# Attention scores of 16-wide heads in sixteen 32x32 array tiles per group, and another order in one pool of buffers

## The chip, the cores and the metric
The kernel runs on one core of a Trainium2 chip. Its time is the device time of one launch in microseconds (us); a profile is one further execution, recorded by the hardware profiler. TensorE (PE) multiplies; it is a systolic array of 128 rows and 128 columns that can be divided into tiles, each of which takes its own weights and its own stream. The profile keeps its weight loads (PEld) apart from its streams (PE). VectorE (DVE), ScalarE (ACT) and GpSimd (POOL) work elementwise beside it, and SyncE (SP) mainly issues transfers.

## The reference, cut to what matters
Two decoder layers over `x` of 8 sequences, 256 rows, 256 features, all in fp32. Layer 0 has self-attention with rotary positions, cross-attention and an expert-choice feed-forward; layer 1 has causal self-attention, cross-attention with a null key, and a feed-forward of eight routed experts and a shared one. The three attentions with heads of 16 compute

```python
# 16 heads of 16; layer 0 self, layer 0 cross (bias b, masked keys), layer 1 self (causal)
scores = einsum('bhqd,bhkd->bhqk', q, k) * scale      # 256 queries x 256 keys a head
attn   = softmax(scores)
out    = einsum('bhqk,bhkd->bhqd', attn, v)           # v of 16 features a head
```

and the feed-forward at the end has the shared expert, whose second weights the other edit touches:

```python
shared_aD = silu(x_aD @ ws1_DF) * (x_aD @ ws3_DF) @ ws2_FD     # F = 704
```

## The kernel before, in words
**Attention units.** `units` is a list of 24: per pair of sequences two self-attentions and two cross-attentions of layer 0, and after those of layer 0 eight causal self-attentions of layer 1. Each unit has a `Core`, and each `Core` runs four steps. `queries` splits a step into `c`, which half of the 16 heads, and `kt`, which 128 of the 256 keys.

**One step.** `scores` makes the group of products named `st` for eight heads (L334). Heads of 16 lie in strips of `HP` = 32 partitions; strip `r` of `kT` holds the keys of two heads side by side in its 32 rows, and `qm` holds the queries twice, `m` = 0 and 1, each time masked to one of the two heads. One matmul per strip thus gives two heads: a contraction of 32 rows, 128 keys as its 128 columns of weights, and 2 x 256 queries as its stream of 512. The four strips are four 32x128 tiles of the array, and each writes its own 2 KB bank of the tile `st`. In the causal units the second key half (`kt` = 1) takes only the second 128 queries, so its stream has 256 columns. There are 24 x 4 = 96 such groups, 16 of them with 256 columns. ACT then turns the group into exponentials in two instructions of two banks each (`pT`, L345), and in causal units POOL blanks the upper triangle (L350). `values` multiplies by the padded values (`o`, L371): eight matmuls on 128x32 tiles. Where `kt` is 1, DVE divides.

**Order.** The pool `scp` that holds `st` has one buffer of four banks, so a group of scores can't start before ACT has read the group before it. The order of the engines is written out by hand under `manual_schedule`, and between the groups stand pieces of the neighbouring units and of the expert layer, put there by `beside(n, k, at, ...)`. The loop is

```python
for k in range(4):
    if k < 3:
        u.core.scores(k + 1)
    elif n + 1 < len(units):
        units[n + 1].core.scores(0)
    run(n, k, True)
    u.core.values(k)
    run(n, k, False)
```

so PE gets the scores of the next step, then (`run(n, k, True)` holds few pieces) the values of this one, then the pieces beside. Those pieces use other tile shapes: `product` (L276) makes two column tiles of 128x64, `product4` (L282) four of 128x32; `transposed` (L291) and the products `hx` (L1079) take the whole array. `lg` is the group of expert logits, four calls of `product4` in one place; `cs`, `rps`, `qk` and `y` are other small groups, `xn` and `xnx` are normalised rows made on DVE, `g` are the gates of the expert layer.

**An fp32 matmul is two.** The profile records two passes for one fp32 matmul of the code, each with its own weight load. The 384 matmuls of L334 are 768 streams and 768 loads in the trace.

**The late stage.** `null_cross_attention` loops `b` over the 8 sequences. At the last `b` it closes the pools of its own weights (`wproj.close()`), opens the pool `late` in their place and calls `load_shared(late)`. That allocates `ws13` and lets `w_in` issue its two DMAs on SP and a small copy on POOL (L1028 to L1030), allocates the two buffers `mid0` and `mid1`, and then `ws2`, each of the three with a small memset on POOL (`ended`, L1035) for its unused end. `w_out` later issues the two DMAs of `ws2` on SP (L1039, L1040), behind the stores that `rest` and `reciprocals` have put on that queue. `hidden_shared` is the first reader of `ws13` (`hx`, L1079); `divide` on POOL and `outward` with its products `wo` (L276) follow. `ws2` is first read from 970.7 us on (`out`, L1663).

The pool takes over addresses that earlier buffers held. In bytes of a partition these were `vx` (values of the last cross-attention, read by the products `ox`, L1470) at 162,464 to 170,656, `wkv_x` at 170,656 to 203,424 and `wq_x` at 203,424 to 211,616. Before the change `ws13` lies at 168,768 to 180,544, over the end of `vx`; then `mid0` from 180,544, `mid1` from 192,832 and `ws2` at 205,120 to 211,264.

Of the kernel before, what the change touches and what calls it, by code (L numbers as in the profile page):

```python
# [29 lines left out]
F32 = mybir.dt.float32  # L30
# [9 lines left out]
P = 128  # L40
B, S, D = 8, 256, 256
NT = B * S // P
H, HD = 16, 16
HP = 32
# [6 lines left out]
NFC = len(FCH)  # L51
# [106 lines left out]
def plain(  # L158
# [4 lines left out]
    nc = tc.nc  # L163
# [100 lines left out]
    def layernorm_T(b, work, mm, bufs=2):  # L264

        xn = work.tile([P, 2, D], F32, tag="xn", name="xn", bufs=bufs)
        mv, rs = norm_stats([x[:, 2 * b + t, :] for t in range(2)], 1e-5, small, "ln")
        for t in range(2):
            last = normed(xn[:, t, :], x[:, 2 * b + t, :], mv, rs, t)
        return last, transposed(xn, work, mm, "xnT", bufs=bufs)  # L270
# [45 lines left out]
    class Core:  # L316
# [9 lines left out]
        def scores(self, step):  # L326


            c, kt, q0 = self.queries(step)
            n = S - q0  # L330
            st = scp.tile([P, 4, 2, S], F32, tag="sc", name="st")
            for r in range(4):
                rows = slice(HP * r, HP * r + HP)
                nc.tensor.matmul(  # L334
                    st[:, r, :, :n],
                    self.kT[rows, c, bass.ts(kt, P)],
                    self.qm[rows, :, c, q0:],
                    start=True,
                    stop=True,
                )  # L340
            pTs = []
            for k in range(2):
                pT = work.tile([P, 2, 2, S], F32, tag="pT", name="pT", bufs=4)
                kb = {} if self.bias is None else {"bias": self.bias[:, kt : kt + 1]}
                nc.scalar.activation(  # L345
                    pT[:, :, :, :n], st[:, 2 * k : 2 * k + 2, :, :n], AF.Exp, scale=self.scale, **kb
                )
                if self.causal:

                    nc.gpsimd.affine_select(  # L350
                        out=pT[:, :, :, :P],
                        in_=pT[:, :, :, :P],
                        compare_op=ALU.is_ge,
                        fill=0.0,
                        base=0,
                        pattern=[[0, 2], [0, 2], [1, P]],
                        channel_multiplier=-1,
                    )
                pTs.append(pT)
            self.exps[step] = pTs  # L360
# [488 lines left out]
    def context(b):  # L849
        t = ctxs.tile([P, CTX // P, S], F32, tag="ctxT", name="ctxT")  # L850
        nc.sync.dma_start(t, a["ctx_T"][b].rearrange("(c p) t -> p c t", p=P))
        return t

    def key_room():
        return kvs.tile([P, nc8, S], F32, tag="kT", name="kTx")
# [61 lines left out]
    for k in range(4):  # L917
# [7 lines left out]
    start = begun + (  # L925
        (0, 2, EARLY), (0, 3, 40), (0, 3, 41), (1, 0, 70), (1, 2, 70),
        (1, 3, 70), (2, 0, 15), (2, 1, 5), (2, 2, 70), (2, 3, 20), (2, 3, 70), (3, 0, 70), (3, 1, 45),
        (3, 2, 70), (3, 3, 85),
    )
# [95 lines left out]
    def w_in(pool, src1, src3, name):  # L1025

        t = pool.tile([P, 2, 2 * FF + tail], F32, name=name, tag=name)
        nc.sync.dma_start(t[:, :, :FF], src1.rearrange("(c p) f -> p c f", p=P))  # L1028
        nc.sync.dma_start(t[:, :, FF + tail :], src3.rearrange("(c p) f -> p c f", p=P))
        nc.gpsimd.tensor_copy(t[:, :, FF : FF + tail], t[:, :, 2 * FF :])  # L1030
        return t

    def ended(t):

        nc.gpsimd.memset(t[tail:, full, :], 0.0)  # L1035
        return t

    def w_out(t, src):
        nc.sync.dma_start(t[:, :full, :], src[: full * P].rearrange("(c p) d -> p c d", p=P))  # L1039
        nc.sync.dma_start(t[:tail, full, :], src[full * P :])  # L1040
        return t
# [5 lines left out]
    shared = {}  # L1047
# [5 lines left out]

    def load_shared(pool):

        shared["ws13"] = w_in(pool, a["L1_ffn_ws1_DF"], a["L1_ffn_ws3_DF"], "ws13")

        shared["mid_s"] = [ended(pool.tile([P, NFC, 2 * S], F32, name=f"mid{i}")) for i in range(2)]
        shared["ws2"] = ended(pool.tile([P, NFC, D], F32, name="ws2"))

    def hidden(mid, first, n, pair, silu):

# [126 lines left out]
    def routed_norm(b, work):  # L1189

        xn = work.tile([P, 2, D], F32, tag="y", name="xne", bufs=1)
        mv, rs = norm_stats([x[:, 2 * b + t, :] for t in range(2)], 1e-5, small, "ln")
        for kept, v in zip(norms[b], (mv, rs)):
            nc.gpsimd.tensor_copy(kept, v)
        for t in range(2):
            normed(xn[:, t, :], x[:, 2 * b + t, :], mv, rs, t)
        return xn

    def routed_rows(b, xn, work):
        transposed(xn, work, mm, "", shared["xnT"][:, :, bass.ts(b, S)])  # L1200
# [87 lines left out]
    def null_cross_attention(phase):  # L1288
# [42 lines left out]
        def sums_of_rows(rows, n, name, apart):  # L1331


            def block(i, j):
                return rows[:, n * j : n * (j + 1), bass.ts(i, P)]

            sw = wsum.tile([P, 4 if apart else 3, n, P], F32, tag=name, name=name)
            s1, s2, s4 = (sw[:, i] for i in range(3))
            s3 = sw[:, 3] if apart else block(1, 0)
            nc.vector.tensor_tensor(s1, block(1, 0), block(1, 1), ALU.add)  # L1340
            nc.vector.tensor_tensor(s2, s1, block(0, 0), ALU.subtract)
            nc.vector.tensor_tensor(s4, block(0, 1), s2, ALU.subtract)
            nc.vector.tensor_tensor(s3, block(0, 0), block(1, 0), ALU.subtract)
            return block(0, 0), block(0, 1), s4, block(1, 1), s1, s2, s3
# [223 lines left out]
        for b in range(B):  # L1568
            more = b + 1 < B
            if more:  # L1570
                ctxT = context(b + 1)
            oT, den, rest = weighted(kT, v, qT)
            if more:
                _, xnT = layernorm_T(b + 1, work, mm, 1)
                if b:
                    xe = routed_norm(b - 1, work)
                of_ctx = sums_of_rows(ctxT, CTX // P // 2, "sw", False)
            else:
                xe = routed_norm(b - 1, work)
                rest()  # L1580

                wproj.close()
                late = ctx.enter_context(tc.tile_pool(name="mids", bufs=1, side="right"))
                load_shared(late)
                sums = phase.enter_context(tc.tile_pool(name="sums", bufs=1, side="right"))
                order.enter_context(tc.manual_schedule(engines={mybir.EngineType.PE}))
            if more:
                order.enter_context(tc.manual_schedule(engines={mybir.EngineType.PE}))
            if b:
                routed_rows(b - 1, xe, work)  # L1590
            if more:
                of_x = sums_of_rows(xnT, 1, "swq", True)
                kT, v, qT = key_room(), value_room(), query_room()
                k7 = seven("k7", of_ctx, w_terms(kv_blocks, 0), kT, False)
                v7 = seven("v7", of_ctx, w_terms(kv_blocks, 1), v, True)
                q7 = seven("q7", of_x, w_terms(q_blocks, 0), qT, False)
                next(k7)
                rest()
            rs, old = reciprocals(b, den, en), en
            if b == 1:  # L1600
                in_range()
            if not more:
                w_out(shared["ws2"], a["L1_ffn_ws2_FD"])
                routing_tables(late)
            if more:

                for made in (k7, k7, v7, k7, k7, k7, v7, v7, q7, v7, q7, v7, v7, q7):
                    next(made)
            else:
                first = hidden_shared(0, pair, lambda n: spare()[:, 0, :n])  # L1610
                for i in range(4):
                    next(first)
                    if i == 0:
                        routed_scores(b - 1)
                shared["of_w"] = sums_of_shared(*(sums.tile([P, full * P], F32, name=f"tws{i}") for i in range(4)))
            divide(oT, rs, (nc.gpsimd, nc.gpsimd if more else nc.vector))
            outward(b, oT, old)
            if more:
                next(q7), next(q7)
                if b:  # L1620
                    routed_scores(b - 1)
                next(q7)
                en = null_key(xnT)
            else:
                for _ in first:
                    pass
            order.close()
# [1230 lines left out]
```

## Time and profile before

| what | value |
|---|---|
| median of 3 runs | 1198.14 us (1196.61 to 1200.52) |
| profiled execution, its own time | 1198.71 us |
| its span | 1197.0 us |
| PE busy | 1135.5 us, 95% |
| weight loads | 706.5 us, 59% |
| DVE, ACT, POOL busy | 47%, 37%, 35% |
| `st` streams (L334) in the chain that ended last | 4% of the span |
| `hx` (L1079) in that chain | 3% of the span |

The span runs from the first to the last recorded instruction; the 1.7 us between it and the execution's own time are start and end. The busy time of PE counts any moment in which at least one stream runs, so streams of several tiles beside each other count once. The row `PEclk` gives the clock that the throttle granted to TensorE in tenths, 9 for nine tenths or more, in 40 slices of 29.9 us. Durations of single instructions are in nanoseconds, and a line of the timeline is a run of equal instructions: its start in us, its length in us, the engine, the line, the operation, the tile of the array (rows by columns), the shape of weights or result, and the count.

### The profile page before, as it was taken

How to read it: one execution, taken by the hardware profiler on the slowest of the kernel's cores; microseconds unless marked ns; L12 is line 12 of the kernel's file. 1: busy time of each engine (PE TensorE's matmuls, PEld its weight loads, DVE VectorE, ACT ScalarE, POOL GpSimd, SP SyncE). 2: the span in 40 equal slices, each digit the busy share in tenths (PEclk: the TensorE clock that was granted, in tenths of full speed). 3: DMA queues.
4: the chain of work that ended last, by engine and by line, in shares of the span. 5: the costliest groups of instructions: out<-in, count | busy, mean ns of one | idle time of the engine just before them, and what ended most of it. 6: DMA issues, size and time to landing. Idle time of an engine off the chain costs nothing.

```text
span 1197.0 us, 31939 instructions
## 1 busy us (share of the span) xinstructions
PE 1135.5 (95%) x13788; PEld 706.5 (59%) x13788; DVE 566.2 (47%) x1564; ACT 447.5 (37%) x696; POOL 417.6 (35%) x482
## 2 busy tenths in 40 slices
PE   6898899998899999999999999999998999999996
PEld 2334444454445454666676767666664576888864
DVE  5465878778685643824241424242324473222213
ACT  3666665665443541314141414141413230222220
POOL 3245365455655730314141414141415114100013
PEclk9999999999999999999999999999998999999999
DMA  7046232130200600020202010101103007799924
GB/s 226 1 133 204 91 119 92 54 122 2 84 2 17 233 3 19 2 54 2 54 2 54 6 50 10 46 19 37 24 15 105 5 30 305 277 414 394 392 73 129
DMA packets 51446, 116.78 MB, mean 98 GB/s; under 512 B 8272, under 2 KB 36416, under 8 KB 46944
## 3 DMA queue, kind: packets, MB, share of 16 engines
q1 hardware_dynamic: 45120, 98.90, 24.0%
q0 software_dynamic: 3456, 12.73, 2.9%
q10 hardware_dynamic: 2720, 3.02, 0.7%
q8 instruction: 110, 1.80, 0.6%
q14 instruction: 40, 0.33, 0.1%
HBM read 104.00 MB, written 27.93 MB: 110 GB/s over the span
## 4 chain that ended last, share of the span: by engine, by line
PE 76%; POOL 7%; issue 6%; DVE 6%; ACT 4%; DMA 1%; SPq 0%; POOLq 0%; ACTq 0%; DVEq 0%
PE h L276 7%; PE k L276 6%; PE v L276 6%; PE wo L276 5%; PE ox L1470 5%; PE stx L1431 5%; PE st L334 4%; PE out L1846 4%; PE o L371 3%; PE out L1663 3%; PE h L1079 3%; PE qk L282 3%; PE q L276 3%; ACT pT L345 2%; PE den L1446 2%
## 5 line engine op out<-in xcount | busy, mean ns | idle before, releaser
L345 ACT ACTIVATE pT<-st 128x1024 f32<-128x1024 f32 (+1 forms) x128 | 110.7, 919 | 64.3 <-PE st L334 64.3
L371 PE MATMUL o<-pT,padv 128*32 128x256 f32 (+1 forms) x1536 | 99.7, 370 | 4.3 <-POOL pT L350 4.2
L371 PEld LDWEIGHTS o<-pT,padv 128*32 128x32 f32 x1536 | 40.6, 109 | 86.2 <-issue 37.5
L1437 POOL TENSOR_TENSOR both<-pTx 128x512 f32<-128x512 f32 x64 | 81.2, 1296 | 29.0 <-ACT pTx L1435 23.8
L276 PE MATMUL h<-xrT,w 128*64 128x128 f32 (+1 forms) x1936 | 87.0, 250 | 0.4 <-issue 0.4
L276 PEld LDWEIGHTS h<-xrT,w 128*64 128x64 f32 x1936 | 84.4, 137 | 3.3 <-issue 1.1
L345 ACT ACTIVATE pT<-st,kbias 128x1024 f32<-128x1024 f32 x64 | 67.9, 1112 | 44.0 <-PE st L334 44.0
L258 POOL TENSOR_TENSOR lnrs<-lnve,mhalf 128x2 f32<-128x2 f32 x48 | 34.7, 723 | 127.8 <-DVE lnve L256 124.1
L1072 DVE TENSOR_TENSOR midr<-sl,h 128x128 f32<-128x128 f32 x102 | 29.4, 288 | 102.5 <-PE h L276 69.9
L1435 ACT ACTIVATE pTx<-stx 128x1024 f32<-128x1024 f32 x64 | 62.1, 1022 | 40.8 <-PE stx L1431 27.7
L1071 ACT ACTIVATE sl<-h 128x128 f32<-128x128 f32 (+1 forms) x114 | 35.4, 311 | 94.7 <-PE h L276 55.7
L334 PE MATMUL st<-qm,kT 32*128 32x512 f32 (+1 forms) x512 | 66.8, 591 | 4.0 <-ACT pT L345 2.0
L1431 PE MATMUL stx<-qTx,kTx 64*128 64x256 f32 x512 | 64.4, 391 | 2.5 <-ACT pTx L1435 2.5
L282 PE MATMUL qk<-l_wqkv,xnT 128*32 128x512 f32 x512 | 63.3, 607 | 0.7 <-ACT xnT L294 0.7
L1470 PE MATMUL ox<-pTx,vx 128*64 128x256 f32 x512 | 62.3, 385 | 0.0
L258 POOL TENSOR_TENSOR lxrs<-lxve,mhalf 128x2 f32<-128x2 f32 x8 | 5.6, 706 | 159.9 <-DVE sc L1210 124.2
L1525 POOL TENSOR_TENSOR oT<-oT,rs 128x512 f32<-128x512 f32 x30 | 37.3, 1273 | 65.0 <-DMA rs<-rd 65.0
L1431 PEld LDWEIGHTS stx<-qTx,kTx 64*128 64x128 f32 x512 | 46.1, 186 | 20.3 <-ACT pTx L1435 7.2
L276 PE MATMUL wo<-wout_x,oT 128*64 128x256 f32 x512 | 58.0, 379 | 0.0
L350 POOL TENSOR_SCALAR_AFFINE_SELECT pT<-pT 128x512 f32<-128x512 f32 x64 | 42.0, 670 | 41.8 <-ACT pT L345 38.7
L1846 PE MATMUL out<-w,midr 128*64 128x256 f32 x408 | 47.1, 379 | 2.7 <-issue 2.7
L1470 PEld LDWEIGHTS ox<-pTx,vx 128*64 128x64 f32 x512 | 33.9, 136 | 26.4 <-issue 12.5
(361 smaller groups left out, 2164.1 us busy)
## 6 DMA issues: line engine op xcount, KB each, us to landing
w<-packs SPq DMA_DIRECT2D x22, 1408.0 KB
w<-packs SPq DMA_DIRECT2D x22, 768.0 KB
rs<-rd SPq DMA_DIRECT2D x16, 512.0 KB
packs<-L_ffn_w_eDF SPq DMA_DIRECT2D x8, 704.0 KB
packs<-L_ffn_w_eDF SPq DMA_DIRECT2D x8, 640.0 KB
packs<-L_ffn_w_eFD SPq DMA_DIRECT2D x8, 640.0 KB
ctxT<-ctx_T SPq DMA_DIRECT2D x8, 512.0 KB
wkv_x<-L_xattn_Wkv POOLq DMA_DIRECT2D x1, 4096.0 KB
```

Of the source, the lines that this page charges most:

```text
L258: nc.gpsimd.tensor_tensor(rs[:, :n], ve[:, :n], mhalf[:, :n], ALU.pow)
L276: nc.tensor.matmul(out[h], lhsT[:, h], rhs, start=start, stop=stop, skip_group_check=True)
L282: nc.tensor.matmul(out[h : h + HP], lhsT[:, h : h + HP], rhs, start=start, stop=stop, skip_group_check=True)
L334: nc.tensor.matmul(st[:, r, :, :n], self.kT[rows, c, bass.ts(kt, P)], self.qm[rows, :, c, q0:], start=True, stop=True,)
L345: nc.scalar.activation(pT[:, :, :, :n], st[:, 2 * k : 2 * k + 2, :, :n], AF.Exp, scale=self.scale, **kb)
L350: nc.gpsimd.affine_select(out=pT[:, :, :, :P], in_=pT[:, :, :, :P], compare_op=ALU.is_ge, fill=0.0, base=0, pattern=[[0, 2], [0, 2], [1, P ...
L371: nc.tensor.matmul(o[HP * j : HP * j + HP, m, q0:], self.v_pad[:, kt, 8 * c + 2 * j + m, :], pTs[j // 2][:, j % 2, m, : S - q0], start=kt ...
L1431: nc.tensor.matmul(st[:, g, kt, :], kT[rows, c, bass.ts(kt, P)], qT[rows, c, :], start=True, stop=True)
L1435: nc.scalar.activation(pT, st, AF.Exp, scale=scale)
L1437: nc.gpsimd.tensor_tensor(both, pT[:, :, 0, :], pT[:, :, 1, :], ALU.add)
L1470: nc.tensor.matmul(o[XD * g : XD * (g + 1), i, :], v[:, kt, 2 * (c2 + i) + g, :], pT[:, g, kt, :], start=kt == 0, stop=kt == 1, skip_group ...
L1846: nc.tensor.matmul(ps[h], mid[:, i, h], sets[k % len(sets)][1][:, i, :], start=i == 0, stop=i == NFC - 1, skip_group_check=True,)
```

## The change
There are two edits. In `scores` the matmul of strip `r` is divided by keys: four matmuls of 32 keys each, of which matmul `j` writes partitions 32 `j` to 32 `j` + 31 of bank `r`. So a group is sixteen 32x32 tiles, four per strip, with the same stream of 512 (or 256) columns each; the code has 1536 matmuls in L334 instead of 384, in the order strip by strip. `skip_group_check` only turns off a check of the compiler's front end.

In `load_shared` the tile `ws2` is allocated first and so lies lowest in the pool: `ws2` at 168,768 to 174,912, `ws13` at 174,912 to 186,688, `mid0` from 186,688, `mid1` from 198,976 to 211,264. The memset on its end moves from `load_shared` to the place where its DMAs are issued.

```diff
             st = scp.tile([P, 4, 2, S], F32, tag="sc", name="st")
             for r in range(4):
                 rows = slice(HP * r, HP * r + HP)
-                nc.tensor.matmul(
-                    st[:, r, :, :n],
-                    self.kT[rows, c, bass.ts(kt, P)],
-                    self.qm[rows, :, c, q0:],
-                    start=True,
-                    stop=True,
-                )
+                for j in range(4):
+                    nc.tensor.matmul(
+                        st[HP * j : HP * j + HP, r, :, :n],
+                        self.kT[rows, c, bass.ts(4 * kt + j, HP)],
+                        self.qm[rows, :, c, q0:],
+                        start=True,
+                        stop=True,
+                        skip_group_check=True,
+                    )
...
     def load_shared(pool):
 
+        shared["ws2"] = pool.tile([P, NFC, D], F32, name="ws2")
         shared["ws13"] = w_in(pool, a["L1_ffn_ws1_DF"], a["L1_ffn_ws3_DF"], "ws13")
 
         shared["mid_s"] = [ended(pool.tile([P, NFC, 2 * S], F32, name=f"mid{i}")) for i in range(2)]
-        shared["ws2"] = ended(pool.tile([P, NFC, D], F32, name="ws2"))
...
             if not more:
-                w_out(shared["ws2"], a["L1_ffn_ws2_FD"])
+                w_out(ended(shared["ws2"]), a["L1_ffn_ws2_FD"])
                 routing_tables(late)
```

## The prediction
> **What bounds the kernel now.** I read the engines' shares first, then the clock row, then the groups by line and shape, then the two places that the change touches.
>
> ```profile
> PE 1135.5 (95%) x13788; PEld 706.5 (59%) x13788; DVE 566.2 (47%) x1564; ACT 447.5 (37%) x696; POOL 417.6 (35%) x482
> ...
> PEclk9999999999999999999999999999998999999999
> ```
>
> TensorE is busy for 95% of the span and its clock is full except near three quarters, so the time is a sum of matmul slots. A score product costs what it keeps the array from the next group, and that is read from the timeline of PE and of its weight loads around one of the 96 score groups:
>
> ```profile
> 202.19 0.25 PE L282 MATMUL cs<-g,ones 128*32 128x16 f32 x9
> 202.38 1.14 PE L334 MATMUL st<-qm,memk 32*128 32x512 f32 x8
> 203.45 1.07 PE L371 MATMUL o<-pT,padv 128*32 128x256 f32 x16
> ...
> 202.37 0.31 PEld L334 LDWEIGHTS st<-qm,memk 32*128 32x128 f32 x8
> 203.44 0.59 PEld L371 LDWEIGHTS o<-pT,padv 128*32 128x32 f32 x16 [0.76 <-issue]
> ```
>
> Four matmuls of the code are eight here: each fp32 product is two passes, with a weight load each. From the first load of `st` to that of `o` are 1.07 us (all full groups agree within a nanosecond or two). The tile view says what they hold:
>
> ```profile
> L334 PEld LDWEIGHTS st<-qm,memk x256: 181/182/184, 52.8 to 279.4; 32*128 32x128 f32 x128
> L334 PE MATMUL st<-qm,memk x256: 587/640/692, 52.8 to 279.8; 32*128 32x512 f32 x128
> ```
>
> A first pass lasts 692 ns and a second 587: the 105 ns between them are the load of 128 columns, with nothing behind which to hide after a change of tile shape. Record by record, the four tiles' loads start 6.7 ns apart, second passes start 427 ns after first ones, and `o` begins 88 ns after the last stream. So a slot is 0.107 + 3 x 0.0067 + 2 x 0.427 + 0.088 = 1.069 us. The 16 groups with 256 columns take 0.644 us, the same less two times 0.213.
>
> Next to it, who makes PE wait, and the chain of waits where the second edit acts:
>
> ```profile
> PE st L334 <- ACT pT L345: 8.5, 11, 1.3
> PE qpsx L547 <- DVE xnx L262: 4.3, 4, 1.1
> PE cs L282 <- DVE g L668: 4.2, 4, 1.4
> ...
> PE hx L1079 <- DMA ws<-L_ffn_ws_DF: 3.4, 1, 3.4
> ...
> 913.52 1.90 PE ox L1470 x16
> 915.43 0.02 SPq L1028
> 915.45 0.04 issue
> 915.49 4.35 DMA ws<-L_ffn_ws_DF
> 919.84 0.14 issue
> 919.98 6.62 PE hx L1079 x8
> ```
>
> The first weights' DMA goes out when the last `ox` ends; PE idles 3.4 us for it and then runs eight 512-column passes in 6.62 us, where the next seven take 3.20: after the idle the clock is halved for them.
>
> **What the Trainium skill says.** "TensorE: Matmul & The Clock Gate", section "LDWEIGHTS (loading the stationary operand)": a load's time follows its columns, columns / 1.2 ns, rows not counting: 107 ns for 128, 27 for 32. The trace agrees: 105 ns for `st`; for `o` (32 columns) first passes of 403 against 379, 24 ns. "TensorEngine Tiling (Array Packing)", "Key Properties": another tile shape drains the array. The trace agrees: 88 ns between any two shapes, whichever they are. The first page's "Measured speedup vs the span model": sixteen tiles cost one matmul plus 4 ns for each further tile, and matmuls stay in program order. Here the step is 6.7 ns (two passes, four instructions), and order isn't kept: the built program has both passes of one tile before the next tile, yet four first passes start together. The same page's opening table: a queue of 64. Here less is seen: PE's sequencer executes the semaphore instruction ahead of a group when mostly 36 to 38 earlier loads and matmuls have not started (at most 44).
>
> **The change part by part.**
>
> *Scores.* Each of 96 groups goes from 4 matmuls to 16, from 16 PE instructions to 64 (4 x 4 tiles, two passes, load and matmul). Streams stay at 2 x 0.427 us, since all sixteen tiles run beside each other; the drain stays at 0.088; the load falls from 0.107 to 0.026 us, as of `o`. The last of sixteen tiles starts T after the first, so the slot becomes 0.968 us + T; the old one is met at T = 0.101. The waits stand on each group's first instruction as before, and the instructions of ACT, DVE, POOL and SP keep their order.
>
> T isn't in the trace for this shape; bounds. From below: dispatch alone, 15 x 6.7 ns = 0.100 (4 ns from the skill: 0.060). From above: supply. The last tile's first pass is instructions 61 and 62 of 64, and these can't all be queued. `lg` is also 64 instructions:
>
> ```profile
> 105.55 0.46 PE L282 MATMUL lg<-gate,xnbT 128*32 128x8 f32 x32
> ...
> 177.09 0.51 PE L282 MATMUL lg<-gate,xnbT 128*32 128x8 f32 x32
> ```
>
> Less one matmul's 0.176 us, 0.28 and 0.33 us lie between first and last start. In the second, instructions come 7.7 ns apart from the start; in the first the burst ends after about 52, and the rest come at 8.3. I take 36 queued and 8.0 ns: T = (62 - 36) x 8.0 = 0.208 us, slot 1.176, +0.107. (44 queued at 7.7 ns: T = 0.139, +0.038; 32 at 8.3: T = 0.249, +0.148.)
>
> 96 x 0.107 = +10.3 us, full and half groups alike. In 5 groups the sequencer passes its semaphore only 0.115 us ahead, with some 14 instructions queued: T = 48 x 8.0 = 0.38, 5 x 0.17 = +0.9 more. Off goes what waits hide: the `st` wait on `pT` does not shrink, because that ACT work starts when the group before ends; the eight on `xnx` and `g` can, by a group or two each: 8 x 0.15 = -1.2. After the score group `o` has 0.85 us of streaming in which to be queued, so its start isn't late. ACT's exponentials, each waiting for the group's last matmul, move with it. Sum **+10.0 us**.
>
> *Second weights.* In the pool the order becomes `ws2`, `ws13`, `mid`: `ws13` no longer overlies `vx` (its start moves up by 6 KB per partition), `ws2` does. But in the two built programs the `ws13` DMA waits for PE's count 5624 before and 6776 after; 96 x 12 = 1152 matmuls are added, so it is the same matmul, the last `ox`. The `ws2` memset stays at its place in POOL's queue, behind those of `mid`, and both `ws2` DMAs stay in SP's, behind the `rd` stores. I cost it at nothing: 0.3 us of POOL that waits for `ox` as its neighbours do, with `ws2` read 50 us later. Were the cover gone, POOL's tables behind it would move by 0.3 us, with slack of microseconds.
>
> The profiled execution took 1198.71 us (span 1197.0 and 1.7 around): 1208.7. The median of the runs lies 0.57 lower: **1208.1 us**.
>
> **Rivals.**
> *Dispatch alone.* The queue holds the group; T = 0.100. For it: at 168.65 `lg` starts all 32 in 0.26 us without thinning. Against: the other two. +0, 1198.
>
> *Faster.* The place is the same 96 slots; it decides when sixteen tiles take under 0.101 us. At the skill's 4 ns a tile, 96 x (0.060 - 0.101) = -4: 1194; the limit of T = 0 gives -9.7: 1188.5. Against it stand the 6.7 ns. A gain could also come if `ws13`'s DMA left early: 3.4 us idle and 6.62 - 3.42 = 3.2 of half clock, of which 5.5 remain since POOL's divisions end at 932.1 and `wo` starts at 937.6. Both programs' waits speak against it: 1192.6 alone, 1202.6 with the scores as forecast.
>
> *Much slower.* Parked second passes fill the window, and the second eight tiles start after a first pass. Then a slot is 0.026 + 0.05 + 3 x 0.427 + 0.088 = 1.45 (half: 0.80): 80 x 0.376 + 16 x 0.16 = +33, 1231. For it: no shape here parks sixteen. Against: in `y` three tiles park some 18 instructions and the fourth still starts. If tiles of one row strip ran after each other it would be over +200.
>
> **How the numbers follow.** Supply 0.50, dispatch alone 0.20, faster 0.22, much slower 0.08. The first's own range is 1201.8 to 1213.5, from 36 against 44 and 32 queued. The whole range, 1190 to 1216, takes in the first two and most of the third. A measurement of this kernel tells about 0.3%, 3.6 us, from no change. Faster takes the third and a little of the second, same most of the second, slower the first and the fourth: 0.22, 0.21, 0.57.
>
> **What would show it.** The score matmuls x3072; loads of 32 columns near 106 ns; from first `st` load to first `o` load 1.17 us; first passes starting over 0.2 us, evenly at first and about 31 ns a tile towards the end; the wait of `hx` for `ws` still 3.4 us. Wrong: slots of 1.07 or less, all sixteen first passes within 0.1 us, second passes ahead of other tiles' first ones, or the `ws` DMA out before `ox` ends.

## The result and the profile after

The changed kernel takes 1201.13 us in the median of 11 runs (1197.79 to 1205.7), the kernel before 1197.66 in as many. The ratio is 1.003 with a 95% interval of 1.0017 to 1.0044: **slower by some 3.5 us**, where the forecast was 10. The profiled execution has a span of 1197.7 us against 1197.0. Single executions of one kernel differ by more than this, so the times below are from the runs, and the traces are used for what they hold group by group.

The engines' shares on the page after:

```profile
PE 1134.3 (95%) x16092; PEld 704.0 (59%) x16092; DVE 566.2 (47%) x1564; ACT 449.0 (37%) x696; POOL 418.4 (35%) x482
```

PE has 2304 more matmuls and as many more loads, and is busy for no longer. The tile view of `st` (durations are shortest, median, longest in ns; the count behind x is that of all records, the one at the end of the shape, is partial):

```profile
L335 PEld LDWEIGHTS st<-qm,memk x1024: 101/103/105, 55.3 to 284.1; 32*32 32x32 f32 x171
L335 PE MATMUL st<-qm,memk x1024: 587/598/612, 55.3 to 284.5; 32*32 32x512 f32 x171
```

The loads last 101 to 105 ns where 106 were expected, and the difference between a first and a second pass is 25 ns instead of 105. The timeline of one group, of PE's loads and of ACT, first before and then after (start, length, engine, line, what):

```profile
60.02 0.31 PEld L334 LDWEIGHTS st<-qm,memk 32*128 32x128 f32 x8 [0.41 <-ACT pT L345]
61.09 0.59 PEld L371 LDWEIGHTS o<-pT,padv 128*32 128x32 f32 x16 [0.76 <-issue]
61.29 2.12 ACT L345 ACTIVATE pT<-st,kbias 128x1024 f32<-128x1024 f32 x2 [1.68 <-PE st L334]
```

```profile
62.68 0.24 PEld L335 LDWEIGHTS st<-qm,memk 32*32 32x32 f32 x32 [0.41 <-ACT pT L347]
63.76 0.59 PEld L373 LDWEIGHTS o<-pT,padv 128*32 128x32 f32 x16 [0.84 <-issue]
64.07 2.12 ACT L347 ACTIVATE pT<-st,kbias 128x1024 f32<-128x1024 f32 x2 [1.69 <-PE st L335]
```

Two things are to be seen. From the first load of `st` to the first of `o` are 1.07 us before and 1.08 after, nearly the old slot and not 1.17. But ACT starts its exponential 1.27 us after that first load before and 1.39 after. PE leaves the group at the old time, and ACT hears of it 0.12 us later. Record by record this is so in nearly every group, with 256 columns too (0.843 against 0.963 us), and it doesn't depend on the slot: where sixteen first passes are spread over 0.167 instead of 0.100 us, ACT still starts at 1.390. The trace also records when PE raises its semaphore: 1.187 us after the first load before and 1.307 after, and ACT starts 0.083 us later both times. So it is PE's report that is late, not ACT's answer to it.

PE's waits after:

```profile
PE st L335 <- ACT pT L347: 10.7, 17, 1.4
PE qpsx L549 <- DVE xnx L262: 4.2, 4, 1.1
...
PE cs L282 <- DVE g L670: 4.1, 5, 1.3
...
PE hx L1081 <- DMA ws<-L_ffn_ws_DF: 3.2, 1, 3.2
```

The wait of `st` for ACT's reading grew from 8.5 to 10.7 us; the wait of `hx` for the weights stands. In 22 groups before and 21 after, the next `st` follows ACT's last reading within 0.06 us: PE and ACT hand one buffer to and fro there, and lateness of ACT is lateness of PE. So the sum is 80 x 0.013 + 16 x 0.004 = 1.1 us for slots and 2.2 for that wait, 3.3 in all. The waits are those of one profiled execution each; what lateness costs is tried by itself further below.

### The profile page after: what moved, and what is told of

Its sections match the earlier page's. It is cut to its first block, busy times and chain, and to the rows that moved or that the text cites. A ratio compares the mean times of both kernels' runs of the same rounds, so it can differ in the third digit from the quotient of the medians.

```text
span 1197.7 us, 36547 instructions
## 1 busy us (share of the span) xinstructions
PE 1134.3 (95%) x16092; PEld 704.0 (59%) x16092; DVE 566.2 (47%) x1564; ACT 449.0 (37%) x696; POOL 418.4 (35%) x482
## 5 line engine op out<-in xcount | busy, mean ns | idle before, releaser
L335 PE MATMUL st<-qm,kT 32*32 32x512 f32 (+1 forms) x2048 | 67.6, 553 | 5.1 <-ACT pT L347 3.3
L389 DVE STREAM_TRANSPOSE by_q<-o 128x512 f32<-128x512 f32 x48 | 34.1, 711 | 30.1 <-PE o L373 29.7
```

The costliest lines, as they stand in the source:

```text
L335: nc.tensor.matmul(st[HP * j : HP * j + HP, r, :, :n], self.kT[rows, c, bass.ts(4 * kt + j, HP)], self.qm[rows, :, c, q0:], start=True, st ...
```

## The experiments

**Theory R.** PE reports finished matmuls one after another, in program order, each 16.6 ns behind the one before. The group carries one semaphore, on its last matmul. It reaches ACT at the end of the first tile's second pass (the profile models these ends), plus 0.082 us, plus 16.6 ns for each matmul up to the last. Before: 1.122 + 0.082 + 4 x 0.0166 = 1.270; after: 1.042 + 0.082 + 16 x 0.0166 = 1.390. These two groups gave the two constants, so each further point tests them. Rivals: **S**, the forecast's supply; **W**, the pool order; **I**, 10 ns for each unit by which the semaphore is raised, as the built program raises it by 16 instead of 4; **T**, the narrow tile itself.

### One edit at a time

The score edit alone:

> The score edit alone, ws2 left where it was. In the changed kernel the slots of `st` grew by only 12 ns in the middle (1.071 to 1.083), but ACT's first exponential starts 1.389 us after the group's first load instead of 1.270, and that distance does not depend on how far the sixteen first passes are spread. Theory R (late release): the whole +3.5 us comes from the scores, about 1.3 from slots and 2.5 from 21 places where PE waits for ACT and ACT waited 0.120 us longer: +3 to +4 us here. Rival W (the pool order costs part): at most +2 here and the rest in the other run. My forecast's theory S (supply): slots of 1.17, +10.

The pool order alone:

> The pool order alone, scores in four tiles. R and the forecast: no difference (within 1 us), the wait of `hx` for `ws` still 3.2 to 3.4 us. W: +1.5 us or more.

The scores alone took 1201.53 us against 1198.58, ratio 1.003 (1.0017 to 1.0042); the pool order alone 1198.63, ratio 1.0004 (0.9992 to 1.0016). In the first, ACT started at 1.390, the slots of full groups had a mean of 1.085, and PE's wait of `st` for `pT` was 11.0 us. In the second all three were as before:

```profile
PE st L334 <- ACT pT L345: 8.3, 10, 1.3
...
PE hx L1079 <- DMA ws<-L_ffn_ws_DF: 3.5, 1, 3.5
```

By their intervals the scores alone lost 2.0 to 5.0 us, where W allowed 2 at most, and the pool order alone -1.0 to 1.9, with no wait moved. So W falls, if only just by the times, and the loss is the scores'.

### Eight tiles

```diff
-                nc.tensor.matmul(
-                    st[:, r, :, :n],
-                    self.kT[rows, c, bass.ts(kt, P)],
+                for j in range(2):
+                    nc.tensor.matmul(
+                        st[64 * j : 64 * j + 64, r, :, :n],
+                        self.kT[rows, c, bass.ts(2 * kt + j, 64)],
```

> Scores in eight tiles of 32 rows and 64 keys, ws2 as before. Slots: load 0.053, eight first passes 6.7 ns apart, so last second pass at 0.055 + 0.427 + 0.047 = 0.529 and slot 0.529 + 0.427 + 0.088 = 1.044 (before 1.071). Release after the group's first load: R with 16.6 ns for each tile, counted from the end of the first tile's second pass (0.482 + 0.587 = 1.069): 1.069 + 0.082 + 8 x 0.0166 = 1.284 us. Rival I (10 ns for each unit of the semaphore's count, added to what four tiles have): 1.270 + 4 x 0.010 = 1.310. Rival T (narrow tiles write late, whatever their number): nearer to 1.389. Time by R: 80 x -0.027 + 16 x -0.027 + 21 x 0.014 = -2.3 us.

The timeline of the same group as above:

```profile
59.78 0.23 PEld L335 LDWEIGHTS st<-qm,memk 32*64 32x64 f32 x16 [0.41 <-ACT pT L347]
60.82 0.59 PEld L373 LDWEIGHTS o<-pT,padv 128*32 128x32 f32 x16 [0.81 <-issue]
61.06 1.11 ACT L347 ACTIVATE pT<-st,kbias 128x1024 f32<-128x1024 f32 x1 [1.66 <-PE st L335]
```

The slot is 1.044 us in nearly every full group, and ACT starts at 1.283 or 1.284 in most: R to a nanosecond, 26 ns from I and over 0.1 from T. The time fell to 1197.26 against 1198.58, ratio 0.9987 (0.9976 to 0.9997), a gain of 0.4 to 2.9 us where 2.3 was expected.

### A buffer for each exponential

The changed kernel with `st` as two buffers of two banks:

```diff
-            st = scp.tile([P, 4, 2, S], F32, tag="sc", name="st")
+            sts = [scp.tile([P, 2, 2, S], F32, tag=f"sc{k}", name=f"st{k}") for k in range(2)]
...
-                    pT[:, :, :, :n], st[:, 2 * k : 2 * k + 2, :, :n], AF.Exp, scale=self.scale, **kb
+                    pT[:, :, :, :n], sts[k][:, :, :, :n], AF.Exp, scale=self.scale, **kb
```

> The changed kernel with `st` as two buffers of two banks each, so that each exponential waits for its own eight tiles and each half of the next group for its own exponential. R: first exponential at 1.042 + 0.082 + 8 x 0.0166 = 1.257 us after the first load (1.389 in the changed kernel), and a next group can begin when the first of two exponentials is done, so in the 21 chained places ACT no longer idles between groups: 2.5 us off for the release and up to the 8.5 us that PE waits for `pT` besides: 1190 to 1196. S: no change of release, 1200.

ACT's first exponential starts at 1.256 to 1.258 us, as R has it. The time is 1197.72 against 1198.58 (0.999, 0.9977 to 1.0003): the loss of the change is gone, and no gain beyond it is shown. The two rows of waits for `pT`:

```profile
PE o L373 <- POOL pT L352: 4.2, 4, 1.8
...
PE st L335 <- ACT pT L347: 0.4, 2, 0.2
```

10.3 us of the wait are gone, but it moved into the group, as PE's loads and ACT show at a chained place:

```profile
51.74 0.18 PEld L335 LDWEIGHTS st<-qm,memk 32*32 32x32 f32 x16 [0.66 <-ACT pT L347]
52.65 0.18 PEld L335 LDWEIGHTS st<-qm,memk 32*32 32x32 f32 x16 [0.73 <-ACT pT L347]
53.67 0.59 PEld L373 LDWEIGHTS o<-pT,padv 128*32 128x32 f32 x16 [0.84 <-issue]
...
50.66 1.94 ACT L347 ACTIVATE pT<-st 128x1024 f32<-128x1024 f32 x2
52.99 2.12 ACT L347 ACTIVATE pT<-st,kbias 128x1024 f32<-128x1024 f32 x2 [0.40 <-PE st L335]
```

The second half starts 0.91 us after the first, when ACT has read its own half. The group then takes 1.94 us instead of 1.08, and PE counts as busy in it.

The same with the four tiles of the kernel before, and with eight:

> The kernel before (four tiles) with `st` as two buffers of two banks. R: first exponential at the first tile's end 1.122 + 0.082 + 2 x 0.0166 = 1.237 us after the group's first load (1.270 before). PE's wait of `st` for `pT` falls from 8.5 us to under 1, as it did with sixteen tiles in halves, and some 5 us of it come back as longer groups whose second half starts later. The sixteen-tile kernel in halves stood at -0.9 us; its slots are 12 to 13 ns longer, 96 x 0.013 = 1.2, and its release 0.020 us later: -2.5 us here, 1196.

> Eight tiles and halves together. R: first exponential at 1.069 + 0.082 + 4 x 0.0166 = 1.217 us, undisturbed slots of 1.044. Time: the four-tile kernel in halves less 96 x 0.027 = 2.6 us: about -5 us against before, 1193. If the gains overlap (both shorten the same wait of PE for ACT), no better than either alone: -2.

The starts of the first exponential are 1.236 to 1.237 and 1.216 to 1.217 us: R again. The times are 1193.59 and 1192.55 us against 1194.67 on the same chip, ratios 0.9984 (0.9976 to 0.9992) and 0.9979 (0.9969 to 0.9988). Both are faster than the kernel before. The first gained 1.1 us where 2.5 were expected. The second has the lowest ratio found, but gained 2.1 us and not 5, about the -2 that its expectation gives for gains that overlap. With four tiles the wait of `st` fell by 8.1 us, and 22 groups with streams of 512 grew by 7.1 together, so that most of it came back. Whether the eight tiles add something to the halves these intervals don't tell.

### Which tile the report waits for

```diff
-            for k in range(2):
+            for k in (1, 0):
                 pT = work.tile([P, 2, 2, S], F32, tag="pT", name="pT", bufs=4)
...
-            self.exps[step] = pTs
+            self.exps[step] = pTs[::-1]
```

> Sixteen tiles in halves, with the exponential of the second half issued first: the first exponential now waits for the eighth to sixteenth tile, whose buffer's semaphore counts 8. R (tiles are reported one after another, 16.6 ns each, in program order): 1.042 + 0.082 + 16 x 0.0166 = 1.389 us after the group's first load. Rival I (the price belongs to the count that a semaphore is raised by): 8 as in the other order, 1.26 to 1.28.

The first exponential started at 1.389 or 1.390 us in 11 full groups and at 1.415 or 1.416 in 59. One group of each kind, the more frequent one first (1.41 and 1.39 us from PE's first load to ACT):

```profile
58.47 0.24 PEld L335 LDWEIGHTS st<-qm,memk 32*32 32x32 f32 x32 [1.91 <-ACT pT L347]
59.88 1.11 ACT L347 ACTIVATE pT<-st,kbias 128x1024 f32<-128x1024 f32 x1 [1.47 <-PE st L335]
...
140.67 0.30 PEld L335 LDWEIGHTS st<-qm,memk 32*32 32x32 f32 x32
142.06 1.11 ACT L347 ACTIVATE pT<-st,kbias 128x1024 f32<-128x1024 f32 x1 [1.77 <-PE st L335]
```

I, with 1.26 to 1.28, falls. The place of the matmul in the group counts, not what its semaphore is raised by. But in most groups R is 0.026 us short. The trace's records of PE's semaphore show what it lacks. In the 59 groups PE raises it twice, at 1.173 us for the first eight tiles and at 1.332 for all sixteen; in the 11 only once, at 1.306 or 1.307 as in the changed kernel. ACT starts 0.083 us after the last raise in both kinds. The other kernels in halves agree: with 2, 4 and 8 matmuls between the two raises they lie 0.059, 0.093 and 0.159 us apart, which is 16.6 ns for each matmul and another 26 to 27. So a second raise in the group costs some 26 ns of its own. The one time, 1199.05, decides nothing.

### Lateness of ACT by itself

```diff
             pTs = []
+            late = work.tile([P, 1], F32, tag="late", name="late")
+            nc.scalar.copy(late, st[:, 0, 0, :1])
```

> The kernel before, with one small ACT copy of a column of `st` ahead of the two exponentials, so that ACT alone is later by its duration d (about 0.2 us by an estimate from ACT's smaller copies) in each of the 96 groups and the matmuls stay as they are. R: lateness of ACT costs its size at the 21 chained places: 21 x d, some +4 us, nothing elsewhere; slots stay at 1.071. If lateness of ACT were hidden everywhere (S): no difference.

The copy overlaps with what follows: it lasts 159 ns, but the exponential starts at 1.320 instead of 1.270, and the second one ends 0.054 to 0.060 later. So d was 0.057, not 0.2, and the 22 chained places should then cost 1.3 us. Slots stayed at 1.071:

```profile
L334 PE MATMUL st<-qm,memk x256: 587/640/692, 52.9 to 280.7; 32*128 32x512 f32 x128
L343 ACT COPY late<-st x96: 158/159/212, 23.3 to 445.6; 128x1 f32<-128x1 f32 x96
```

The wait of `st` for `pT` grew by 1.5 us to 10.0, and the time to 1196.49 against 1194.67, ratio 1.0018 (1.0009 to 1.0028), 1.1 to 3.3 us. With no matmul changed, ACT's lateness alone costs time, and the interval holds the 1.3.

### Twice the matmuls, half as long

```diff
-            for r in range(4):
+            for m in range(2):
+              for r in range(4):
...
-                        st[HP * j : HP * j + HP, r, :, :n],
+                        st[HP * j : HP * j + HP, r, m, :n],
...
-                        self.qm[rows, :, c, q0:],
+                        self.qm[rows, m, c, q0:],
```

> The changed kernel with every one of the sixteen tiles given its 512 columns in two matmuls of 256 (first all sixteen tiles for one of the two heads of a strip, then all for the other): 32 matmuls, 128 recorded instructions a group. R: reports begin when the first matmul ends (0.242 + 0.374 = 0.616 us after the first load, as in the groups with 256 columns), 32 of them take 0.531, so the last would be at 0.616 + 0.082 + 0.531 = 1.229, and at the earliest after its own end near 1.142 + 0.082 + 0.017 = 1.24: the exponential starts at 1.24 to 1.27, earlier than the 1.389 of sixteen matmuls, though there are twice as many. A price for each matmul whatever its length would give 1.5 to 1.65; a price of the tile's shape 1.39. Supply: at 16.6 ns for each matmul the 32nd is there at (32 - 9) x 0.0166 = 0.38, before its tile is free at 0.455: slots 1.07 to 1.10. At the forecast's 8.0 ns for each recorded instruction it comes at (126 - 36) x 0.008 = 0.72: slots 1.24 and +13 us. Time by R: slots +1.2, release nothing: within 2 us of before.

1236.42 us against 1198.04, ratio 1.0326 (1.0301 to 1.0352): the largest miss.

```profile
59.90 1.01 PEld L336 LDWEIGHTS st<-qm,memk 32*32 32x32 f32 x64 [1.75 <-ACT pT L348]
61.32 0.59 PEld L374 LDWEIGHTS o<-pT,padv 128*32 128x32 f32 x16 [0.41 <-issue]
61.49 1.11 ACT L348 ACTIVATE pT<-st,kbias 128x1024 f32<-128x1024 f32 x1 [1.64 <-PE st L336]
```

The loads of one group, 0.24 us before, now stretch over 1.01, and the slot is 1.424. In the records sixteen first passes start within 0.10 us as in the changed kernel, the seventeenth at 0.457 when its tile is free, and the load of the eighteenth at 0.647. That is 0.031 after the first matmul's end (0.242 + 0.374 = 0.616). From there one matmul starts every 16.6 ns. The groups with half as many columns agree: there the first matmul ends at 0.403 and the eighteenth's load is at 0.434. So PE appears to hold about seventeen matmuls that it has not reported, and to take a new one for each report. Supply binds after all, but counted in what is unreported, and sixteen matmuls in a group just fit. Whether the limit counts matmuls, passes or recorded instructions isn't told apart: each matmul here is two passes and four instructions. The excess of 0.353 x 80 + 0.353 x 16 = 34 us explains most of the 38; the rest was not traced. ACT starts at 1.594: the last matmul's end of 1.496 + 0.082 + 0.017 = 1.595. R's price of the last report holds; my slot, made with a supply in instructions, does not.

## Why the prediction was wrong

- **The direction** was right, but in part by luck: of the 3.3 us that the traces account for, 1.1 came by the way forecast, longer slots, and 2.2 by a wait that was taken as fixed. 1201.13 lies in the whole range, and just below the forecast's own part of it. The size was not right, +3.5 us against +10.0. Two steps failed, in opposite directions.
- **T, "I take 36 queued and 8.0 ns: T = (62 - 36) x 8.0 = 0.208 us".** Measured: 0.100 to 0.115 in most groups, at most 0.167, so the slot is 1.070 to 1.084 in most and 1.136 at the worst, mean +0.013 instead of +0.107. T was mis-sized by two. In the burst of the first `lg` the recorded matmul passes come four in 32 ns, and each pass has its own load: 8.0 ns is the step of a pass, 4.0 that of a recorded instruction. Only its last eight passes thin out, to some 14 ns each. The other `lg` has 332 ns for 31 steps, 10.7 a pass or 5.4 an instruction, and not 7.7. I counted the queue in instructions and multiplied by the step of a pass. Where sixteen tiles do run short, they start 16.6 ns apart, four instructions each, 4.15 ns. With that, T = 26 x 4.15 = 0.108, slot 1.076. This fits, but it does not show that 36 was the right count: in 25 of 78 full groups all sixteen tiles start 6.7 ns apart and nothing runs short, as the forecast's own signs of being wrong have it. The rival "dispatch alone", given 0.20, was right on the slots; it stood in the same trace. (The range given with T is also off by a sum: 96 x 0.148 with the short leads and the waits is about +13.7, so 1212 at the top and not 1213.5.)
- **"Its start isn't late"** (of `o`) was right. What I left out is the next engine: "ACT's exponentials, each waiting for the group's last matmul, move with it" takes for granted that the report comes with the end. It comes 0.12 us later with sixteen matmuls, which made +2.2 us at the wait that I had named and costed at nothing more. No rival had it. All `st` groups of before have four tiles, but other groups of that trace show the number: PE raises its semaphore 14 ns after the last modelled end where one tile runs (`hx`), 24 where two run side by side (`ox`) and 44 where four do (`st`, `o`). That is 10 ns for each further tile, the 16.6 of a report less the 6.7 between the tiles' starts, and by that sum some 165 ns for sixteen; measured are 164.
- **Loads, streams, drain.** Right: second passes of the first tile start at 0.455 instead of 0.535, and `o` begins 0.088 after the last stream. The load did save 0.080 us; the sixteen starts took it back, since they last 0.100 or more against 0.020. That the drain is 88 ns "whichever" the shapes is too even: by the same working it is 88 after streams of 512 columns, 94 after 256 and 97 after the 8 of `lg`.
- **The five groups with a short lead, +0.9.** Wrong. Nine full groups have slots from 1.105 to 1.136 us, with an excess over 1.071 of 0.5 us together, but only three of the five are among them, all at 1.105. The six longest, 1.128 to 1.136, follow groups of `cs` and had their semaphore passed 0.48 us and more ahead. So the lead of the sequencer doesn't decide alone; what else does was not tried for these groups.
- **The waits on `xnx` and `g`, -1.2.** Wrong: from 4.3 and 4.2 to 4.2 and 4.1.
- **The second weights at nothing.** Right: 1.0004, and the wait of `hx` unchanged. (The 3% of the chain that the table of before gives to `hx` are all of L1079; `hx` has 17.1 us of it, 1.4% of the span.)
- **"Much slower", parked second passes**, was wrong here; the size that it feared came with twice the matmuls, where the loads wait for reports.
- **The Trainium skill.** That a load follows its columns ("TensorE: Matmul & The Clock Gate", "LDWEIGHTS (loading the stationary operand)") is confirmed at 32, 64 and 128 columns (first passes of `st` longer by 25, 52 and 105 ns than second ones). That matmuls keep program order stands on that page in the section "The mechanism", not where the prediction puts it; the trace differs, with second passes from 0.455 us and the first passes of all sixteen tiles within 0.115 in most groups. Its 4 ns for each further tile ("TensorE: Matmul & The Clock Gate", "Measured speedup vs the span model") are not what fp32 tiles show in any of these kernels: 6.7 ns between starts, and 16.6 where they run short.

## What to carry to other kernels

Ask of a group of matmuls not only when PE can go on but when the reader hears of it: here one fp32 matmul more in the group put off the semaphore by 16.6 ns, at 32, 64 and 128 columns of weights alike. So with one buffer the best division was the one with eight tiles: the load is half as long as with four, and the report only 0.014 us later. Where two engines hand one buffer to and fro, a split by readers takes the wait away, but here most of it came back inside the group; that a quicker reader would keep the gain was not tried. And before a spacing is multiplied by a count, see that both count the same thing.

## What was not expected of the hardware

- The last report of a group comes at the first matmul's end + 0.082 us + 16.6 ns for each matmul, or at its own end + 0.082 + 0.017 if that is later. The two constants come from 1.270 and 1.389 us; four more groupings of full streams (1.284, 1.257, 1.237 and 1.217) and the short streams (1.594) fit within 1 ns at their most frequent values. By the semaphore's records 0.083 us of this are the way from PE's raise to ACT's start. Where a group raises the semaphore twice, the second raise is another 26 ns later. It was seen in fp32 matmuls of two passes only; whether the 16.6 ns are two passes of 8.3 wasn't tried.
- About seventeen fp32 matmuls are in flight before the first is reported, as the kernel with twice the matmuls shows; the next one's load starts 0.031 us after the first one's end, and after that one every 16.6 ns.
